# Graph attention over gathered rows: whole-array columns and value transposes, and another order of the first layer's step

## The chip, the cores and the metric

The kernel runs on one NeuronCore of a Trainium2 chip. The metric is the device time of one execution in microseconds, as the median of several runs. The engines are TensorE (PE, with its weight loads PEld), VectorE (DVE), ScalarE (ACT), GpSimd (POOL) and SyncE (SP), and 16 DMA engines that move data. [...]

## The reference

Eight graphs share one adjacency matrix of 2048 nodes; each node has 64 features. A graph attention layer with four heads is followed by a second one with one head, a layer norm, the residual and another layer norm. Scores are the inner products of a layer's features, masked by the adjacency matrix with the diagonal added:

```python
mask = graph + jnp.eye(N, dtype=graph.dtype) > 0
h = jnp.einsum('bnc,hdc->bhnd', x, Wh)
out_h = _gat_layer(h, mask[None, None], bh[None, :, None, :])      # softmax over masked h.h, times h, plus b
cat = jnp.transpose(out_h, (0, 2, 1, 3)).reshape(B, N, H * D)
z = jax.nn.leaky_relu(cat, negative_slope=0.2)
h2 = jnp.einsum('bnk,dk->bnd', z, Wo)
out2 = _gat_layer(h2, mask[None], bo)
z2 = jax.nn.leaky_relu(out2, negative_slope=0.2)
out = layernorm(z2) * gamma + beta                                 # then layernorm(x + out)
```

Here B is 8, N 2048, H 4, D and C 64, and all is float32.

## The kernel before

The adjacency matrix is sparse but for its first rows. The kernel (`fast_kernel`; a general one stands behind it for inputs that do not fit) treats the first 56 nodes, the hubs, densely, and puts the other 1992 into 166 sets of 12 nodes. For every set VectorE picks, from keys that hold a bit mask of the set's members and a node number, the up to 128 neighbours that the set has in all. These neighbours' rows are gathered from a table in device memory by an indirect DMA that GpSimd issues, and attention is done on the 128 rows alone.

There are three stages. The hub stage (to about 140 us) loads x, writes the first table, transposes x into `xT` (`turn_x`) and computes the hubs' attention, while GpSimd and VectorE turn the adjacency matrix into keys and pick neighbours. The second stage is the loop that the change is about: the first layer, 83 groups of two sets (about 145 to 625 us). The third is the second layer, from a second table that the loop writes.

One group of the first layer passes through these functions, each in another step of the software pipeline, so that a step works on some eight groups at once:

- `gather` (L797): two indirect DMAs bring 128 rows of 4 x 130 numbers each; a row holds, for each of four pairs of graphs, a one, 128 features and a one. `own_rows` (L808, L811) copies the members' own columns out of `xT` for two groups at a time, on GpSimd.
- `columns` (L819) multiplies the own columns with `gram` (Wh transposed times Wh, per head, 64x64 for each of two graphs, block diagonal in 128x128), and `keep_columns` (L826) copies the result to `y` on ScalarE. So a score is a gathered row times y.
- `turn` (L514) transposes the gathered rows, and ScalarE copies them to `xTg` (L1045).
- `scores` (L836): 16 matmuls, weights 64x128 from `xTg`, 48 columns each (12 members by 4 heads); `weigh` (L842) subtracts the mask on VectorE, `lift` (L849) takes the exponential on ScalarE.
- `values` (L861): 16 matmuls, exponentials as weights, rows of 65 numbers (features and a one, which gives the softmax's sum); `invert` (L871, L872) divides on VectorE.
- `turn_values` (L880) transposes the result, `keep_values` (L886) copies it, `project` (L538) applies the heads' Wh, `leaky` (L525) and `leak` (L530) are the leaky ReLU, `second_maps` (L895) applies Wo, `keep_own` (L900) and `store_own` (L905) keep the result, `second_rows` (L911) transposes it, and `keep_rows` (L915, L918) adds the bias and writes the second table.

The order on each engine is the order of the calls: nothing rearranges it. Semaphore waits are added where a tile is written or read by another engine. PSUM is used as four tiles of two banks each, with the tags S, C, T and O, each with one buffer. Before the change each has one reader: S is read by VectorE (scores), T by ScalarE (columns, transposed rows), C by ScalarE (project, transposed values) and O by VectorE (second_maps, values, second_rows). Most matmuls of a step use a part of the array: "64*64" in a profile's row is a tile of 64 rows and 64 columns, four of which are in the array at once. A float32 matmul stands in the profile as two records, a transpose as one.

`some` pops jobs of neighbour picking for later sets from a list and issues them on VectorE; `more` loads and converts a piece of the adjacency matrix; `make_keys` makes keys; `hub_later` finishes the hubs in three jobs for each half; `load_own` and `add_beta` prepare a third table (x + beta) for the end of layer two, by SP's DMAs and GpSimd.

Of the kernel before, what the change touches and what calls it, by code (L numbers as in the profile page):

```python
# [44 lines left out]
HUB = 56  # L45
# [314 lines left out]
def fast_kernel(ctx: ExitStack, tc: tile.TileContext, x, adj, Wh, bh, Wo, bo, gamma, beta, out, flag):  # L360
# [29 lines left out]
    rowp = stage.enter_context(tc.tile_pool(name="rowp", bufs=12))  # L390
# [118 lines left out]
    def turn(tp, rows, j=0):  # L509

        for q in range(Q):
            c0 = (j * Q + q) * 64
            for r in range(2):
                nc.tensor.transpose(tp[:, r, c0:c0 + 64], rows[half(r), q, 1:1 + P], ident[half(r), half(r)])  # L514

    def turn_whole(tp, rows):

        for q in range(Q):
            nc.tensor.transpose(tp[:, q * P:(q + 1) * P], rows[:, q, 1:1 + P], ident)  # L519
# [12 lines left out]
    def project(ot, cat, n):  # L532

        for hp in range(HP):
            for s in range(2):
                for j in range(2):
                    h = 2 * hp + j
                    at = nc.tensor.matmul(cat[half(j), s, hp * n:(hp + 1) * n], whT[half(s), h * D:(h + 1) * D],  # L538
                                          ot[half(s), h, :], start=True, stop=True)
        return at  # L540
# [47 lines left out]
    def turn_x(i):  # L588
        tp = two(f"px{i}")
        turn(tp, xrow[i])  # L590
        nc.scalar.copy(xT[:, :, i * P:(i + 1) * P].rearrange("c q (r n) -> c r q n", r=2),
                       tp[:, :, :Q * 64].rearrange("c r (q n) -> c r q n", q=Q))
# [141 lines left out]
    def pick(r):  # L734
# [7 lines left out]
        def top(src, dst, last):  # L742
            todo.append(lambda: nc.vector.max(out=dst, in_=src))
            if not last:
                todo.append(lambda: nc.vector.match_replace(out=src, in_to_replace=dst, in_values=src, imm_value=-1.0))

        for j in range(ns):
            for i in range(KEEP // 8):
                k = j * KEEP + i * 8
                top(kv[:, j, :], cand[:, k:k + 8], i == KEEP // 8 - 1)  # L750
# [7 lines left out]
        for i in range(P // 8):  # L758
            top(cand, best[:, i * 8:(i + 1) * 8], i == P // 8 - 1)
# [35 lines left out]
    def gather(table, s, layer, new, behind=None):  # L795
        t = rows[layer, s] = new(f"g{layer}_{s}")
        g = nc.gpsimd.indirect_dma_start(out=t.rearrange("n q c -> n (q c)"), out_offset=None, in_=table,  # L797
                                         in_offset=bass.IndirectOffsetOnAxis(ap=index[:, s:s + 1], axis=0))
        if behind is not None:
            tc.add_manual_dep(g.ins, behind.ins.name, mybir.DependencyInfo(mybir.DependencyClass.Sync, mybir.DependencyReason.DATA),  # L800
                              reason="the gather's turn")

    def own_rows(m):

        t = held["x", m] = work.tile([P, 2 * GM], F32, tag="xo", name=f"xo{m}", bufs=2)
        v = t.rearrange("c (b s q k) -> c b s q k", b=2, s=2, q=Q)
        src = xT[:, :, HUB:].rearrange("c q (k s) -> c s q k", s=NS)
        nc.gpsimd.tensor_copy(v[:, 0], src[:, 4 * m:4 * m + 2])  # L808
        b0 = min(4 * m + 2, NS - 2)
        for r in range(2):  # L810
            nc.gpsimd.tensor_copy(v[half(r), 1], src[half(1 - r), b0:b0 + 2])  # L811

    def columns(g, tp):

        t = held["x", g // 2]
        for k in range(2):
            for r in range(2):
                for p in range(2):
                    nc.tensor.matmul(tp[half(p), r, k * GM:(k + 1) * GM], gram[half(r), g % 2 * 2 + k, half(r)],  # L819
                                     t[half(r), (p ^ r) * GM:((p ^ r) + 1) * GM], start=True, stop=True)  # L820

    def keep_columns(g, tp):
        if g % 2 == 0:
            held["y", g // 2] = work.tile([P, 2 * GM, H], F32, tag="yg", name=f"y{g // 2}", bufs=2)
        h0 = g % 2 * 2
        nc.scalar.copy(held["y", g // 2].rearrange("p (b n) h -> p b n h", b=2)[:, :, :, h0:h0 + 2],  # L826
                       tp[:, :, :2 * GM].rearrange("p b (k n) -> p b n k", k=2))

    def scores(g, sp):
        xt = held.pop(("T", 1, g))  # L830
        y = held["y", g // 2].rearrange("p n h -> p (n h)")
        for j in range(2):
            for q in range(Q):
                for p in range(2):
                    c0 = ((g % 2) ^ p) * GM * H + (j * Q + q) * M
                    at = nc.tensor.matmul(sp[:, p, (q * 2 + j) * M:(q * 2 + j + 1) * M], xt[half(p), j, q, :],  # L836
                                          y[half(p), c0:c0 + M], start=True, stop=True)
        return at
# [12 lines left out]
    OW = D + 2  # L851

    def values(g, op):
        e = es[g % 2]
        rw = [rows.pop((1, 2 * g + j)) for j in range(2)]
        for q in range(Q):
            for j in range(2):
                for p in range(2):
                    c0 = (p * 8 + q * 2 + j) * M
                    o0 = q * OW + p  # L860
                    at = nc.tensor.matmul(op[half(p), j, o0:o0 + K1], e[:, c0:c0 + 64], rw[j][:, q, sums(p)], start=True, stop=True)  # L861
                    if (q, j, p) == (1, 1, 1):
                        midway = at
        return midway

    def invert(g, op):
        v = op[:, :, :Q * OW].rearrange("a j (q c) -> a j q c", q=Q)
        osb = held["o", g] = work.tile([P, 2, Q, D], F32, tag="osb", name=f"osb{g}")
        r = rall[:, g, :].rearrange("a (j q) -> a j q", j=2)
        for p in range(2):  # L870
            nc.vector.reciprocal(r[half(p)], v[half(p), :, :, p * K1])  # L871
        nc.vector.tensor_tensor(osb, v[:, :, :, 1:K1], r.unsqueeze(3).to_broadcast([P, 2, Q, D]), OP.mult)  # L872

    def turn_values(g, pt):

        osb = held.pop(("o", g)).rearrange("a j q c -> a (j q c)")
        for w in range(4):
            for p in range(2):
                mine = slice(p * 64, p * 64 + M)
                at = nc.tensor.transpose(pt[:, p, w * M:(w + 1) * M], osb[mine, w * P:(w + 1) * P], ident[mine, mine])  # L880
        return at

    def keep_values(g, pt):

        ot = held["ot", g] = work.tile([P, H, GM], F32, tag="ot", name=f"otb{g}")
        nc.scalar.copy(ot.rearrange("c h (p m) -> c p h m", p=2), pt.rearrange("c p (m h) -> c p h m", h=H))  # L886
# [14 lines left out]

    def store_own(g):

        t = held["own", g]
# [3 lines left out]
    def second_rows(g, pr):  # L908
        t = held.pop(("own", g))
        for r in range(2):  # L910
            nc.tensor.transpose(pr[:, r, :], t[half(r)], ident[half(r), half(r)])  # L911

    def keep_rows(g, pr):
        r = rowts[g % 4]
        nc.vector.tensor_tensor(r[:GM, 1:1 + P].rearrange("n (p d) -> n p d", p=2), pr, bob[:GM], OP.add)  # L915
# [63 lines left out]
    for i in range(NB):  # L979
# [16 lines left out]
        for t in range(2):  # L996
# [12 lines left out]
            some(6)  # L1009
# [4 lines left out]
    for g in range(3):  # L1014
# [23 lines left out]
    for i in range(-4, NG + 4):  # L1038
        if i >= 1 and slow and len(slow) % 3:
            slow.pop(0)()  # L1040
        sp = one(f"s{i + 1}", "S")
        scored = scores(i + 1, sp) if 0 <= i + 1 < NG else None
        if 0 <= i + 2 < NG:
            t = held["T", 1, i + 2] = work.tile([P, 2, Q, P], F32, tag="xTg", name=f"xTg{i + 2}", bufs=2)
            nc.scalar.copy(t.rearrange("c j q (r n) -> c r (j q) n", r=2),  # L1045
                           held.pop(("tp", i + 2)).rearrange("c r (m n) -> c r m n", n=64))
        cat = one(f"cat{i}", "C")
        if 0 <= i - 2 < NG:
            project(held.pop(("ot", i - 2)), cat, GM)
            held["z", i - 2] = leaky(cat, GM, f"z{i - 2}")  # L1050
        if 0 <= i + 1 < NG:
            weigh(i + 1, sp)
        coming = i + LOOK if i > -3 else NG
        if coming < NG:
            gather(table1, 2 * coming, 1, rows_tile, scored)
        if turns():
            some(1)
        if i >= 0:
            if slow and len(slow) % 3 == 0:
# [4 lines left out]
        tp = one(f"t{i + 3}", "T")  # L1064
        if 0 <= i + 4 < NG + NG % 2:
            columns(i + 4, tp)
            keep_columns(i + 4, tp)
        if 0 <= i + 1 < NG:
            lift(i + 1)
        op = one(f"o{i}", "O")  # L1070
        if 0 <= i - 3 < NG:
            second_maps(i - 3, op[:, 0, 264:264 + GM])
        midway = values(i, op) if 0 <= i < NG else None
        if coming < NG:
            gather(table1, 2 * coming + 1, 1, rows_tile, midway)
        if 0 <= i - 4 < NG:
            second_rows(i - 4, op[:GM, :, 360:424])
        if 0 <= i - 2 < NG:
            leak(held["z", i - 2])
        if 0 <= i - 3 < NG:  # L1080
            keep_own(i - 3, op[:, 0, 264:264 + GM])
            store_own(i - 3)
        if i + 6 < NG and i % 2 == 0 and i >= -2:
            own_rows((i + 6) // 2)
        if i >= 10 and (i - 10) // 6 * 2 + (i - 10) % 6 // 2 <= NV and (i - 10) % 6 < 4:
            (add_beta if i % 2 else load_own)((i - 10) // 6 * 2 + (i - 10) % 6 // 2)
        if 0 <= i < NG:
            invert(i, op)
        if 0 <= i - 4 < NG:
            keep_rows(i - 4, op[:GM, :, 360:424])  # L1090
        for _ in range(6 if i < 0 else 3 if i < 16 else 2):
            if not turns():
                some(1)
        if not picks:
            ready = done
        if not picks and not todo3 and done < NS:
            picks = pick(2)
            done = NS
        assert i + 1 + LOOK >= NG or 2 * (i + 1 + LOOK) + 1 < ready
# [357 lines left out]
```

## Time and profile before

| | |
|---|---|
| runs | 906.34, 915.76, 911.70 us; median 911.7 |
| profiled execution | 906.34 us; its span 904.5 us |
| TensorE clock granted, mean | 0.924 |
| first layer's loop, first to last subtraction L842 | 156.1 to 611.7 us |
| gathers (L797) | 332 of 994 ns each on GpSimd |
| DMA | 145 MB, mean 160 GB/s |

In the profile a row such as "L836 PE MATMUL s<-y,xTg 64*128 64x48 f32 x2656" names the line, the engine, the operation, the tile written and those read, the tile of the array (weights' rows by columns), the moving operand's size, and how many such records there are. A share of busy time is an average over stages; what bounds a stage is read from that stage's windows and from the chain of waits in it.

### The profile page before, as it was taken

What the parts mean: (1) busy time and instruction counts of PE and PEld (TensorE: products, weight loads), DVE (VectorE), ACT (ScalarE), POOL (GpSimd) and SP (SyncE); (2) the same over time, 40 slices, a digit from 0 to 9 for tenths busy, and PEclk for the clock granted to TensorE, in tenths of its full rate; (3) what the DMA queues carried; (4) which work ended last, traced back from release to release, by engine and by line L of the source; (5) the groups of instructions that cost most, each with busy time, mean ns of one, the idle gap of its engine ahead of it and who ended that gap; (6) DMA issues with size and microseconds to landing.
All of it is one profiled execution on the core that took longest, in us unless ns stands there. A gap on an engine that the chain in (4) does not pass through costs nothing.

```text
span 904.5 us, 40409 instructions
## 1 busy us (share of the span) xinstructions
PE 769.5 (85%) x17676; PEld 698.0 (77%) x17676; DVE 615.1 (68%) x1369; ACT 513.4 (57%) x878; POOL 487.5 (54%) x696
## 2 busy tenths in 40 slices
PE   2896776889889999999999999994799999998720
PEld 2675565778779999999999999993699989997720
DVE  3347867447677787767655556655338899999993
ACT  2332243345446666666666666662477887887721
POOL 5643140436555566655556665631777777777300
PEclk9998797669999999999999999997799999999965
DMA  8786350335444555555445455431888888888521
GB/s 176 227 239 201 107 149 4 98 101 146 112 129 130 143 142 148 149 156 143 136 127 153 140 152 153 138 83 43 255 273 248 268 263 270 270 252 249 170 49 30
DMA packets 81787, 145.11 MB, mean 160 GB/s; under 512 B 30146, under 2 KB 46466, under 8 KB 81602
## 3 DMA queue, kind: packets, MB, share of 16 engines
q0 software_dynamic: 26720, 88.55, 34.3%
q1 hardware_dynamic: 37842, 49.65, 18.0%
q10 hardware_dynamic: 17040, 4.25, 2.5%
q8 instruction: 140, 2.29, 1.0%
q14 instruction: 45, 0.37, 0.1%
HBM read 123.91 MB, written 18.48 MB: 157 GB/s over the span
## 4 chain that ended last, share of the span: by engine, by line
PE 61%; DVE 14%; DMA 11%; issue 4%; ACT 4%; POOL 2%; SPq 2%; DVEq 0%; POOLq 0%; ACTq 0%
PE s L836 15%; PE o L861 8%; DMA g<-table,index 5%; PE t L514 4%; PE t L819 4%; PE o L895 4%; PE cat L538 4%; DMA raw<-in_adj_dram 4%; PE t L519 4%; PE s L1156 3%; PE o L1188 3%; PE sh L1300 2%; PE cat L880 2%; PE e L1167 2%; PE o L911 2%
## 5 line engine op out<-in xcount | busy, mean ns | idle before, releaser
L797 POOL DMA_INDIRECT g<-table,index x332 | 330.1, 994 | 136.6 <-issue 54.3
L836 PE MATMUL s<-y,xTg 64*128 64x48 f32 x2656 | 169.6, 280 | 0.8 <-DVE rowt L660 0.8
L836 PEld LDWEIGHTS s<-y,xTg 64*128 64x128 f32 x2656 | 164.0, 197 | 1.7 <-DVE rowt L660 1.2
L842 DVE TENSOR_TENSOR e<-s,mask 128x768 f32<-128x768 f32 x83 | 79.3, 956 | 50.7 <-PE s L836 47.5
L525 ACT ACTIVATE z<-cat,bhp 128x192 f32<-128x192 f32 x166 | 60.9, 418 | 84.6 <-PE cat L538 79.3
L861 PE MATMUL o<-g,e 128*64 128x65 f32 x2656 | 96.5, 228 | 0.0
L519 PE MATMUL t<-ident,g 128*128 128x128 f32 x664 | 82.0, 277 | 12.8 <-DMA g<-table,index 12.8
L861 PEld LDWEIGHTS o<-g,e 128*64 128x64 f32 x2656 | 91.3, 144 | 0.6 <-issue 0.4
L811 POOL COPY xo<-xT 64x96 f32<-64x96 f32 x84 | 30.1, 359 | 113.5 <-DMA g<-table,index 101.5
L1343 ACT COPY xTg<-t 128x1024 f32<-128x1024 f32 x83 | 80.1, 1016 | 17.1 <-PE t L519 16.5
L1045 ACT COPY xTg<-t 128x1024 f32<-128x1024 f32 x83 | 84.4, 1017 | 2.9 <-PE t L514 2.9
L519 PEld LDWEIGHTS t<-ident,g 128*128 128x128 f32 x664 | 75.0, 143 | 14.2 <-issue 9.1
L849 ACT ACTIVATE e<-e,shifts 128x768 f32<-128x768 f32 x83 | 78.1, 941 | 0.7 <-DVE e L842 0.7
L886 ACT COPY otb<-cat 128x384 f32<-128x384 f32 x83 | 39.8, 479 | 66.5 <-PE cat L880 66.5
L604 ACT ACTIVATE e<-e,shifts 128x896 f32<-128x896 f32 x32 | 33.3, 1042 | 74.6 <-DVE e L601 65.2
L687 POOL TENSOR_SCALAR a<-raw 120x1024 bf16<-120x1024 int32 (+1 forms) x34 | 38.4, 1133 | 65.2 <-DMA raw<-in_adj_dram 36.4
L900 DVE COPY own<-o 128x96 f32<-128x96 f32 x83 | 21.3, 257 | 69.6 <-PE o L911 64.2
L530 DVE SCALAR_TENSOR_TENSOR z<-z 128x384 f32<-128x384 f32 x83 | 49.7, 599 | 27.3 <-ACT z L525 23.9
L819 PE MATMUL t<-xo,gram 64*64 64x96 f32 x1328 | 54.8, 260 | 14.2 <-DVE keys L715 5.3
L826 ACT COPY y<-t 128x384 f32<-128x384 f32 x83 | 43.5, 524 | 28.6 <-PE t L819 28.4
L514 PE MATMUL t<-ident,g 64*128 64x64 f32 x1328 | 57.9, 230 | 1.9 <-ACT y L826 1.9
L872 DVE TENSOR_TENSOR osb<-o,rall 128x512 f32<-128x512 f32 x83 | 57.4, 692 | 2.9
(171 smaller groups left out, 1488.3 us busy)
## 6 DMA issues: line engine op xcount, KB each, us to landing
raw<-in_adj_dram SPq DMA_DIRECT2D x32, 480.0 KB
table<-xb SPq DMA_DIRECT2D x22, 256.0 KB
xr_s<-table SPq DMA_DIRECT2D x21, 256.0 KB
g<-table,index POOLq DMA_INDIRECT x332
table<-x SPq DMA_DIRECT2D x16, 260.0 KB
x<-in_x_dram ACTq DMA_DIRECT2D x32, 128.0 KB
table<-rowt SPq DMA_DIRECT2D x166, 24.4 KB
xb<-in_x_dram SPq DMA_DIRECT2D x164, 24.0 KB
```

The lines of the kernel that those rows point to most:

```text
L514: nc.tensor.transpose(tp[:, r, c0:c0 + 64], rows[half(r), q, 1:1 + P], ident[half(r), half(r)])
L519: nc.tensor.transpose(tp[:, q * P:(q + 1) * P], rows[:, q, 1:1 + P], ident)
L525: nc.scalar.activation(z[:, hp], cat[:, :, hp * n:(hp + 1) * n], AF.Identity, bias=bhp[:, hp:hp + 1], scale=1.0)
L797: g = nc.gpsimd.indirect_dma_start(out=t.rearrange("n q c -> n (q c)"), out_offset=None, in_=table, in_offset=bass.IndirectOffsetOnAxis(ap ...
L819: nc.tensor.matmul(tp[half(p), r, k * GM:(k + 1) * GM], gram[half(r), g % 2 * 2 + k, half(r)], t[half(r), (p ^ r) * GM:((p ^ r) + 1) * GM] ...
L836: at = nc.tensor.matmul(sp[:, p, (q * 2 + j) * M:(q * 2 + j + 1) * M], xt[half(p), j, q, :], y[half(p), c0:c0 + M], start=True, stop=True)
L842: nc.vector.tensor_tensor(e[:, :16 * M].rearrange("p (a q n) -> p a q n", a=2, q=Q), sp[:, :, :8 * M].rearrange("p a (q n) -> p a q n", q= ...
L849: nc.scalar.activation(e[:, :16 * M], e[:, :16 * M], AF.Exp, bias=shifts[:, 0:1], scale=1.0)
L861: at = nc.tensor.matmul(op[half(p), j, o0:o0 + K1], e[:, c0:c0 + 64], rw[j][:, q, sums(p)], start=True, stop=True)
L872: nc.vector.tensor_tensor(osb, v[:, :, :, 1:K1], r.unsqueeze(3).to_broadcast([P, 2, Q, D]), OP.mult)
L1045: nc.scalar.copy(t.rearrange("c j q (r n) -> c r (j q) n", r=2), held.pop(("tp", i + 2)).rearrange("c r (m n) -> c r m n", n=64))
L1343: nc.scalar.copy(t, tp)
```

## The change

In `turn_x` the transposes use the whole array. `own_rows` copies the own columns of a pair of groups in one copy, without the second, swapped half. `columns` becomes two matmuls over 128 rows with the block-diagonal gram and 192 columns, which go into tile C. `turn_values` becomes four transposes of 112 rows into free columns of tile O, where `values` also writes, and `keep_values` two copies. `second_maps` and `second_rows` write into C, and `second_rows` is one whole transpose. So C is read by ScalarE (project, columns) and VectorE (second_maps, second_rows), O by VectorE (values) and ScalarE (transposed values). The scores and the transposes of gathered rows stay as they were in size, but the latter are split in two parts with `turn_values` between them. The gathers lose their explicit waits for `scores` and for the middle of `values`; the pool of gathered rows has 10 buffers for 12. The pipeline is shorter: project runs one step after values, second_maps two, second_rows three (two, three and four before). A picking job is now a maximum together with its replacement, two jobs a step from step 0 on (later three in two steps), where single operations stood, six a step before step 0 and then three or two. `load_own` and `add_beta` begin at step 30, not 10.

```diff
-    rowp = stage.enter_context(tc.tile_pool(name="rowp", bufs=12))
+    rowp = stage.enter_context(tc.tile_pool(name="rowp", bufs=10))
...
     def turn_x(i):
         tp = two(f"px{i}")
-        turn(tp, xrow[i])
+        turn(tp[:, 0, :], xrow[i])
...
     def own_rows(m):
-        v = t.rearrange("c (b s q k) -> c b s q k", b=2, s=2, q=Q)
-        nc.gpsimd.tensor_copy(v[:, 0], src[:, 4 * m:4 * m + 2])
-        for r in range(2):
-            nc.gpsimd.tensor_copy(v[half(r), 1], src[half(1 - r), b0:b0 + 2])
+        nc.gpsimd.tensor_copy(t[:, :w * 48].rearrange("c (s q k) -> c s q k", s=w, q=Q), src)
...
         for k in range(2):
-            for r in range(2):
-                for p in range(2):
-                    nc.tensor.matmul(tp[half(p), r, k * GM:(k + 1) * GM], gram[half(r), g % 2 * 2 + k, half(r)],
-                                     t[half(r), (p ^ r) * GM:((p ^ r) + 1) * GM], start=True, stop=True)
+            nc.tensor.matmul(cat[:, k, 2 * GM:2 * GM + n], gram[:, g % 2 * 2 + k, :], held["x", g // 2][:, :n], start=True, stop=True)
...
         for w in range(4):
-            for p in range(2):
-                mine = slice(p * 64, p * 64 + M)
-                at = nc.tensor.transpose(pt[:, p, w * M:(w + 1) * M], osb[mine, w * P:(w + 1) * P], ident[mine, mine])
+            nc.tensor.transpose(turned(op)[:, w, :], osb[:112, w].rearrange("a s c -> a (s c)"), ident[:112, :112])
...
-        for r in range(2):
-            nc.tensor.transpose(pr[:, r, :], t[half(r)], ident[half(r), half(r)])
+        nc.tensor.transpose(pr, held.pop(("own", g)), ident)
```

The loop's body after the change, cut to its order:

```python
for i in range(-4, NG + 3):
    scores(i + 1, sp); weigh(i + 1, sp)
    hub_later's jobs, all but the first of three
    project(i - 1) into cat; leaky(i - 1)
    xTg(i + 2) <- tp; lift(i + 1)
    values(i, op); invert(i, op)
    gather(2 * (i + 5)); gather(2 * (i + 5) + 1)
    own_rows for i + 6, i + 7 (even i); load_own or add_beta (from i = 30)
    leak(i - 1)
    slots of some, hub_later's first job, more(1), make_keys
    second_maps(i - 2, cat); second_rows(i - 3, cat); columns(i + 4, cat)
    keep_own(i - 2); keep_rows(i - 3)
    some(2)
    keep_columns(i + 4, cat)
    turn_halves(tp, first set of i + 3)
    turn_values(i, op); keep_values(i, op)
    turn_halves(tp, second set of i + 3)
```

## The prediction

> **What bounds the kernel now.** I read the page's busy shares first, then windows of the first layer's loop, then the chain of waits inside one of its steps, then who waits for whom.
>
> ```profile
> PE 769.5 (85%) x17676; PEld 698.0 (77%) x17676; DVE 615.1 (68%) x1369; ACT 513.4 (57%) x878; POOL 487.5 (54%) x696
> ```
>
> TensorE has the largest share, but the average mixes stages. The change touches the first layer's loop (83 groups; the scores' subtraction L842 runs 83 times, from 156.1 to 611.7 us) and, with one line, the hub stage before it. So I asked for the loop's windows (columns: busy time and instructions of PE, PEld, DVE, ACT, POOL; then granted clock, DMA share, GB/s):
>
> ```profile
> 156.00:205.00 49.00, 42.55 (x670) 37.77 (x670) 22.64 (x58) 18.84 (x32) 21.07 (x29) 0.66 0.33 94
> 205.00:275.00 70.00, 61.84 (x1421) 56.23 (x1419) 50.25 (x129) 36.67 (x66) 39.43 (x61) 0.93 0.45 126
> 275.00:430.00 155.00, 153.83 (x3969) 145.12 (x3965) 117.96 (x310) 103.54 (x183) 93.16 (x143) 1.00 0.52 146
> 430.00:600.00 170.00, 168.31 (x4250) 157.73 (x4250) 100.20 (x234) 111.06 (x197) 103.21 (x159) 0.99 0.50 141
> ```
>
> From 275 us on PE is 99% busy at full clock and no other engine is above 77%: PE is the bound. Before 205 us the clock is 0.66, so the same work takes longer there. The chain of waits of one undisturbed step says what PE's time consists of:
>
> ```profile
> 461.74 1.79 PE s L836 x32
> 463.53 0.49 PE cat L538 x16
> 464.02 0.33 PE t L819 x16
> 464.35 0.48 PE o L895 x8
> 464.83 0.93 PE o L861 x32
> 465.76 0.19 PE o L911 x2
> 465.95 0.54 PE t L514 x16
> 466.49 0.24 PE cat L880 x8
> 466.73 1.79 PE s L836 x32
> ```
>
> The chain never leaves PE, and the step lasts 466.73 - 461.74 = 4.99 us; most steps in the trace are 4.94 apart. L538 and L819 are the same 16 instructions of 64x64 by 96 columns, but the first costs 0.49 and the second 0.33: L538 is first after the scores, which run as 64x128 tiles. So a switch between tile shapes costs 0.16. L895 repeats it: its 8 records cost 0.48, as 4 pairs at the pace of L819's quartets (0.33 / 4) cost 0.33, and they follow a switch to 128x64. The third switch, back to 64x128, is in L911. Three switches a step now.
>
> Steps 273.3 to 602.6 us are 64; at 4.94 they would take 316, so 13 us are lost, mostly in every second step. Steps 156.1 to 273.3 are 16, 117 us in place of 79: 38 lost. Who waits:
>
> ```profile
> POOL xo L811 <- DMA g<-table,index: 99.2, 34, 3.8
> ...
> PEld t L819 <- POOL xo L811: 7.6, 18, 2.2
> ```
>
> The second copy of own_rows waits on POOL until the gathers in flight have landed, and L819 then waits for it.
>
> **The change, part by part.** In the new step PE issues: scores (64x128), project (64x64), values and second_maps (128x64), second_rows and columns (128x128), turn_halves of the first set (64x128), turn_values (128x128), turn_halves of the second set (64x128). That is six switches, not three.
> - Scores, project: as now, 1.79 + 0.49.
> - Values take over the switch into 128x64 from second_maps: 0.93 + 0.16 = 1.09; second_maps 0.33.
> - Full-array transposes. The second layer has them: its chain shows
>
> ```profile
> 748.89 0.59 PE e L1167 x4
> 749.47 1.75 PE t L519 x16
> ```
>
>  1.75 / 16 = 0.11 each, and four of them after a switch 0.59 (4 x 0.11 + 0.15, the switch again). turn_values becomes four such: 0.59 for 0.24. second_rows becomes one after a switch: 0.26 for 0.19.
> - Columns: 2 matmuls with 192 columns over 128 rows, four records for sixteen. No 192-column pass is in the trace. The nearest is the hub scores' L598 (224 columns), whose pairs of passes start 0.19 apart in the trace (the chain gives x8 0.96 with the switch: (0.96 - 0.16) / 4 = 0.20). By columns, 0.163 a pass, 0.65 in all, for 0.33 now. Lower bound 4 x 0.11 (the 128-column transposes), upper 4 x 0.20; I take 0.65, as 192 is nearest to 224.
> - turn_halves: the 16 records of L514 take 0.49 in the steps beside this one; split in two by turn_values, each half pays a switch: 2 x (0.245 + 0.16) = 0.81.
>
> [...]
>
> Sum of the new step: 1.79 + 0.49 + 1.09 + 0.33 + 0.26 + 0.65 + 0.59 + 0.81 = 6.01, against 4.94 now: +1.07, over 82 steps **+88 us**.
>
> What covers the other engines, in time from the step's start. invert waits for values (done near 3.5), takes 0.41 + 0.69 (L871, L872) and ends near 4.75; turn_values is reached at 5.0: cover 0.25. second_maps writes the bank pair that leaky reads, so it waits for ScalarE: project ends near 2.4, leaky takes 0.73, so 3.25; PE arrives at 3.4: cover 0.15. turn_halves needs the xTg copy (1.02) behind leaky: 4.3, PE arrives at 4.75. keep_columns now waits for VectorE too, because keep_own and keep_rows read the same pair of banks: leak, own, rows end near 5.85, keep_columns (0.52) and keep_values, now two copies (2 x 0.37, as L525's 0.73 for two of that size), end at 7.2; the next project comes at 6.01 + 1.95 = 7.96. Behind the waiting keep_columns only keep_values is queued. All hidden, so nothing is charged; if cover fails by 0.2 a step it costs 16 us.
>
> [...]
>
> VectorE: 0.96 + 0.41 + 0.69 + 0.56 + 0.26 + 0.28 = 3.16 a step, and now two picks of a maximum and a replacement each (0.43 + 0.09 + 0.41, some 0.98 with gaps) for the first 22 steps, where single operations stood: 5.1, under 6.01. POOL: two gathers at 1.28 with their issue, own_rows one copy, add_beta 1.26 every other step: under 4. The gathers now wait for values, at 3.5, are issued by 6.1 and, by the 3.8 us that the copy L811 waits behind them at most, land by 10; turn_halves wants them two steps on, at 16.8. Ten row buffers instead of twelve are covered by that. load_own and add_beta start 20 steps later; SP issues load_own's eight DMAs in 3.35 us (at 463.9), every second step, so the two DMAs of keep_rows behind them still fit a step and have four row buffers; table3 is read only in layer two. The jobs of hub_later move behind the scores and their subtraction: to_table then waits for the subtraction, about 1.1 us, where now the scores wait for its row (L660, 0.4 us); it runs twice, 1 to 2 us, within the rounding of what follows.
>
> What is removed: L811's wait. The 13 us of 64 steps hold 2 for a step with a table of indices (6.8 us, stays); the other 11 are its, and so are 5 of the step at 222 us (10.1 us long: PE idle 1.98 behind L811, then half clock): **-16**. The first steps' other 33 us (hub_later, make_keys, half clock) stay; some ten steps at clock 0.66 make the added 1.07 half as dear again: +5. turn_x: four full transposes for eight halves, 0.44 for 0.24, and a switch more, 16 times 0.36 = 6; the hub stage waits for ScalarE and VectorE too, so half: +3. The drain is a step shorter: -2.
>
> Total: 88 - 16 + 5 + 3 - 2 = **+78**. The profiled execution took 906.3 (span 904.5 and 1.8 around it): 984. It was the fastest of three; their median is 911.7, and from that it would be 990. I say **985**, nearer the execution that the sum is made from.
>
> **Rivals.**
> 1. PE is bound as above, with small terms off: 962 to 1000. 66%.
> 2. The thin covers fail: second_maps, turn_halves or turn_values wait 0.2 to 0.4 each step, and idle brings half clock as it did at 222 us. For it: covers of 0.15 to 0.25, and 0.56 us of leak that once took 1.4 at 299 us. Against: the PE queue has slack after a wait. 985 + 16 to 33 = 1001 to 1018. 14%.
> 3. The new switches are cheaper (full-height tiles load their weights early): three at 0 in place of 0.16 is -39: 946; half of that 966. Against: L1167 pays 0.15 right there. 14%.
> 4. Not slower: a switch's cost is no drain but the order of banks, and vanishes wherever the next operation has another pair of banks. Then all six are free, also the three paid now: 6.01 - 0.96 = 5.05, +0.11 x 82 = 9, with -16 and +6: 905, or 911 from the median. It decides if a switch costs under 0.03 (six of them are then 0.2 a step). Against: L538 and L819 write different banks and only the first pays. 4%. That the change does otherwise than it says (2%) I exclude by the built order, which has these instructions.
>
> **The numbers.** The range 950 to 1010 holds rival 1, half of 2 and most of 3. Faster by over 1% (about what a measurement of this kernel tells from no change): 0.03, the better half of 4 and the unknown; within 1%: 0.03; slower: 0.94.
>
> **What would show it.** Right: steps 5.9 to 6.1 us apart between 300 and 600 us, PE still 98% busy at clock 1.00, columns near 0.65, turn_values near 0.59, two pieces of turn_halves near 0.4 each, no wait of POOL's xo copy for gathers. Wrong: columns at 0.33; switch steps without the extra 0.15; PE idle before second_maps, turn_halves or turn_values; VectorE over 95% in the first 45 steps; or a clock under 0.9 after 275 us.

## The result, and the profile after

The changed kernel takes 956.09 us (median of 4 runs, 952.12 to 959.59) where the kernel before takes 913.73 in the same measurement (4 runs, 906.34 to 920.58): ratio 1.049, 95% interval 1.040 to 1.058. Its profiled execution took 958.55 us, with a span of 956.7 beside 904.5 before: +52.2 where the forecast had +78. The profiled execution of before was its fastest run, so the medians lie only 42 us apart. On another chip the sign was the other one; that is in the experiments (f1 and f2).

The page of the kernel after, busy time by engine:

```profile
PE 832.6 (87%) x16189; PEld 721.6 (75%) x16189; DVE 611.8 (64%) x1369; ACT 514.8 (54%) x961; POOL 464.1 (49%) x612
```

TensorE has 1,487 matmul records fewer (a float32 matmul makes two) and is busy 63 us longer. The windows of the first layer's loop, columns as before:

```profile
156.00:205.00 49.00, 44.28 (x684) 37.98 (x680) 24.19 (x62) 20.69 (x44) 20.09 (x27) 0.80 0.34 93
205.00:275.00 70.00, 66.22 (x1215) 56.51 (x1210) 55.15 (x142) 36.90 (x75) 33.22 (x47) 1.00 0.41 111
275.00:430.00 155.00, 154.33 (x2959) 135.16 (x2961) 106.10 (x288) 88.78 (x182) 73.17 (x97) 1.00 0.43 118
430.00:600.00 170.00, 169.33 (x3248) 148.09 (x3244) 88.86 (x215) 98.41 (x201) 89.63 (x114) 1.00 0.50 139
```

PE is 99.6% busy at full clock from 275 us on, and gets through 2959 records in 155 us where before got through 3969. Ahead of 275 us its clock is higher than before's (0.80 for 0.66, 1.00 for 0.93). The chain of waits through one step:

```profile
464.63 1.77 PE s L825 x32
466.40 0.49 PE cat L538 x16
466.89 1.08 PE o L850 x32
467.98 0.33 PE cat L884 x8
468.31 0.24 PE cat L894
468.55 0.65 PE cat L811 x4
469.20 0.40 PE t L514 x8
469.60 0.53 PE o L867 x4
470.13 0.39 PE t L514 x8
470.52 1.77 PE s L825 x32
```

It never leaves PE. Read down the column beside the forecast's terms: scores 1.77 (1.79), project 0.49, values 1.08 (1.09), second_maps 0.33, second_rows 0.24 (0.26), columns 0.65, halves 0.40 and 0.39 (0.405 each), turn_values 0.53 (0.59). The step is 5.89 us (6.01), and 57 of the 60 steps from 18 to 77 lie within 0.12 of it. Last, who waits for whom between 200 and 640 us (total, times, longest):

```profile
POOL g L797 <- PE o L850: 194.5, 74, 5.8
...
ACT y L817 <- DVE rowt L898: 56.4, 72, 4.3
```

The gathers wait for values (`L850` here), and keep_columns (`L817`) waits for VectorE, as the forecast had it; nothing on PE waits behind either. No wait of the copy of own_rows for gathers is left.

So the span's +52.2 comes from these stretches (us; a step is the distance between two of the scores' subtractions):

| stretch | before | after | difference | the forecast implied |
|---|---|---|---|---|
| to the first subtraction | 156.1 | 154.1 | -2.0 | +3 |
| steps -1 to 14 | 117.2 | 115.7 | -1.5 | 16 x 1.07 + 5 - 5 = +17 |
| steps 15 to 80 | 338.4 | 390.1 | +51.7 | 66 x 1.07 - 11 = +60 |
| behind the last subtraction | 292.8 | 296.8 | +4.0 | -2 |

### The profile page after: what moved, and what is told of

Read it like the earlier page. It is cut to its first block, busy times and chain, and to the rows that moved or that the text cites. A ratio compares the mean times of both kernels' runs of the same rounds, so it can differ in the third digit from the quotient of the medians.

```text
span 956.7 us, 37570 instructions
## 1 busy us (share of the span) xinstructions
PE 832.6 (87%) x16189; PEld 721.6 (75%) x16189; DVE 611.8 (64%) x1369; ACT 514.8 (54%) x961; POOL 464.1 (49%) x612
## 4 chain that ended last, share of the span: by engine, by line
PE 70%; DVE 12%; DMA 4%; ACT 4%; issue 4%; POOL 2%; SPq 2%; ACTq 1%; DVEq 0%; POOLq 0%
PE s L825 16%; PE o L850 9%; PE t L514 7%; PE cat L811 6%; PE o L867 5%; PE cat L538 4%; PE t L519 4%; PE s L1137 3%; PE cat L884 3%; PE o L1169 3%; PE cat L894 2%; PE e L1148 2%; PE sh L1281 2%; ACT xTg L1324 1%; SPq L1252 1%
## 5 line engine op out<-in xcount | busy, mean ns | idle before, releaser
L825 PE MATMUL s<-y,xTg 64*128 64x48 f32 x2656 | 164.1, 274 | 0.0
L825 PEld LDWEIGHTS s<-y,xTg 64*128 64x128 f32 x2656 | 158.6, 192 | 0.1
L525 ACT ACTIVATE z<-cat,bhp 128x192 f32<-128x192 f32 x166 | 60.8, 418 | 154.1 <-PE cat L538 154.1
L850 PE MATMUL o<-g,e 128*64 128x65 f32 x2656 | 99.1, 229 | 0.0
L850 PEld LDWEIGHTS o<-g,e 128*64 128x64 f32 x2656 | 87.3, 142 | 10.0 <-issue 0.4
L514 PEld LDWEIGHTS t<-ident,g 64*128 64x128 f32 x1328 | 54.8, 140 | 33.1 <-issue 20.9
L514 PE MATMUL t<-ident,g 64*128 64x64 f32 x1328 | 77.2, 238 | 2.4 <-issue 2.4
L817 ACT COPY y<-cat 128x384 f32<-128x384 f32 (+1 forms) x80 | 40.9, 511 | 61.9 <-DVE rowt L898 59.0
L857 DVE RECIPROCAL rall<-o 64x8 f32<-64x8 f32 x166 | 34.0, 205 | 58.3 <-PE o L850 57.1
L811 PE MATMUL cat<-xo,gram 128*128 128x192 f32 (+1 forms) x320 | 65.7, 328 | 0.0
L811 PEld LDWEIGHTS cat<-xo,gram 128*128 128x128 f32 x320 | 53.7, 202 | 0.2 <-issue 0.2
L1169 PE MATMUL o<-g,es 128*32 128x65 f32 x2656 | 48.2, 224 | 5.0 <-DVE y_s L1192 4.5
```

The lines of the kernel that those rows point to most:

```text
L525: nc.scalar.activation(z[:, hp], cat[:, :, hp * n:(hp + 1) * n], AF.Identity, bias=bhp[:, hp:hp + 1], scale=1.0)
L811: nc.tensor.matmul(cat[:, k, 2 * GM:2 * GM + n], gram[:, g % 2 * 2 + k, :], held["x", g // 2][:, :n], start=True, stop=True)
L1169: nc.tensor.matmul(op[t * 32:(t + 1) * 32, f, k * W2 + p:k * W2 + p + K1], e[:, 2 * q + p, k, :], rw[:, q, sums(p)], start=(a == 0 and k = ...
```

## The experiments

The theory (A in what follows): PE's own time sets the step, and the added time is in the switches between tile shapes and in the columns. The rivals go by run. Runs e1 to e4 shared a chip (before: 920.73 us median, 13 runs, 911.29 to 929.98). The record doesn't say whether the first measurement fell on it too; "the first chip" below stands for both.

**e1, columns alone.** Before, with whole-array columns and one copy in own_rows (still into tile T):

```diff
-                    nc.tensor.matmul(tp[half(p), r, k * GM:(k + 1) * GM], gram[half(r), g % 2 * 2 + k, half(r)],
-                                     t[half(r), (p ^ r) * GM:((p ^ r) + 1) * GM], start=True, stop=True)
+            nc.tensor.matmul(cat[:, k, 0:n], gram[:, g % 2 * 2 + k, :], held["x", g // 2][:, :n], start=True, stop=True)
```

> The kernel before with one part of the change: columns as two whole-array matmuls of 192 columns (into tile T, as before), and own_rows as one copy; nothing else. Theory A (PE is the bound, a switch of tile shape costs 0.15, a pass of 192 float32 columns 0.163): columns cost 0.65 in place of 0.33 and there is one switch more (64x64 to 128x128 to 128x64), so steps lie 5.4 apart in place of 4.94, +39 us over 82 steps; the copy no longer waits for gathers, -16; so 23 us slower than before, ratio 1.02 to 1.03. Rival B (a switch costs nothing in itself, the added time comes from the waits between engines): step 5.26, +26 - 16 = +10. Rival C (the lost waits weigh more than the array work): faster than before, ratio under 1.00, with the half-clock stretches before 275 us shorter.

Measured: 932.44 us (931.16 to 933.58), ratio 1.012 (1.004 to 1.019). That is 11.7 us between the medians, which by itself would be rival B's +10; the span, 931.3, is 26.8 above before's profile. The steps decide: 5.46 us, flat (A: 5.4, B: 5.26), and the copy of own_rows waits for no gather. From its chain of waits:

```profile
459.21 0.49 PE cat L538 x16
459.70 0.85 PE t L814 x4
460.55 0.48 PE o L887 x8
```

Four records take 0.85 where sixteen took 0.33: 0.65 of work, as in the kernel after, and 0.20 for the switch. That is +0.52 a step, and the wait it takes away gives part of it back. Against e4 below, which lacks that wait too, e1 is 33.8 us slower (medians), and its steps 15 to 80 take 359.5 us for 326.7: 0.50 a step.

**e2, turn_values ahead of both halves.** After, with the first `turn_halves` moved behind `turn_values`: two switches less, as turn_values follows columns in the same shape and the second half follows the first; and less time for VectorE's invert.

```diff
-            turn_halves(tp, rows[1, 2 * (i + 3)], 0)
         if 0 <= i < NG:
             turn_values(i, op)
             keep_values(i, op)
         if 0 <= i + 3 < NG:
+            turn_halves(tp, rows[1, 2 * (i + 3)], 0)
             turn_halves(tp, rows[1, 2 * (i + 3) + 1], 1)
```

> The changed kernel with one thing moved: turn_values stands right after columns, and both parts of turn_halves follow it. Theory A: two of six switches go (turn_values stays in the 128x128 shape, the second half follows the first), 0.27 a step, but PE then reaches turn_values at 4.67 after the scores' start, when VectorE's division is just ending (4.70 in the trace), so 0.1 to 0.2 of it becomes a wait: steps 5.72 to 5.80 in place of 5.89, 8 to 14 us faster than the changed kernel; without any wait 22. Rival B (switches are free): the wait alone remains, steps 6.0 to 6.1, 8 to 16 us slower than the changed kernel.

Measured: 952.32 us (944.75 to 960.38), ratio to before 1.036 (1.027 to 1.046); steps 5.84.

```profile
465.09 0.65 PE cat L811 x4
465.74 0.03 issue
465.77 0.60 PE o L867 x4
466.37 0.64 PE t L514 x16
```

The two halves together take 0.64 where they took 0.40 + 0.39: a switch is worth 0.15. But turn_values now takes 0.60, for the wait for invert that the first half had covered: between 200 and 640 us its weight loads wait 69 times for VectorE's division, 22.0 us in all, where the kernel after has no such wait. So the step gains 0.05 only, outside of what either theory gave, nearer to A. The first half did cover invert there, as the forecast had it.

**e3, values turned in row tiles.** After, with `turn_values` as eight transposes in row tiles and one `keep_values` copy, as before the change (values and invert then lay out tile O as before, too):

```diff
-            nc.tensor.transpose(turned(op)[:, w, :], osb[:112, w].rearrange("a s c -> a (s c)"), ident[:112, :112])
+            for p in range(2):
+                mine = slice(p * 64, p * 64 + M)
+                nc.tensor.transpose(turned(op)[:, p, w * M:(w + 1) * M], osb[mine, w * P:(w + 1) * P], ident[mine, mine])
```

> The changed kernel with turn_values again as eight transposes of 48 rows in 64x128 tiles, into tile O (one bank for each row half), and keep_values as one copy; the order is unchanged. Theory A: turn_values costs 0.24 in place of 0.53 and the two switches around it go, so turn_halves, turn_values, turn_halves cost 0.39 + 0.24 + 0.25 = 0.88 in place of 1.32: steps 5.45 in place of 5.89, 36 us faster than the changed kernel, about 920. Rival B (only the transposes' width counts): 0.44 becomes 0.24, steps 5.69, 16 us faster.

Measured: 920.70 us (10 runs, 912.91 to 925.94), ratio to before 1.001 (0.996 to 1.005), some 35 us below the 956.09 of the kernel after, which was measured apart. Steps 5.46. From its chain:

```profile
469.25 0.65 PE cat L811 x4
469.91 0.39 PE t L514 x5
470.30 0.24 PE o L868 x5
470.53 0.26 PE t L514 x7
```

turn_values takes 0.24 for 0.53, and the second half 0.26 for 0.39: a switch less at each of the two places, and less work in the first. The step is 0.43 shorter, so rival B (5.69) falls; with e1's 0.52 that is 0.95, all of 5.89 - 4.94. (Some records are missing in this view; the times are those of whole groups.)

**e4, the swapped copy on VectorE.** Before, with only the engine of the copy L811 changed:

```diff
-            nc.gpsimd.tensor_copy(v[half(r), 1], src[half(1 - r), b0:b0 + 2])
+            nc.vector.tensor_copy(v[half(r), 1], src[half(1 - r), b0:b0 + 2])
```

> The kernel before with one thing moved: the two swapped copies of own_rows run on VectorE, where they wait for no gather; GpSimd keeps the first copy. Theory A (the copy's wait behind the gathers made columns late, and the pause left PE at half clock for some us): 11 us of the 64 steps after 273 us and 5 us of the step at 222 us go, so 12 to 18 us faster than before, ratio 0.98 to 0.985, and no step after 300 us over 5.3 but the one with a table of indices. Rival B (the lost time of the early steps also hangs on that wait): 25 to 35 us faster, with the half-clock stretches between 145 and 205 us shorter as well. Rival C (VectorE's queue makes the copies late in its place): no gain.

Measured: 898.66 us (890.97 to 906.16), ratio 0.970 (0.960 to 0.979); steps are 4.94 flat from step 48 on. The 22 us between the medians lie between A's 12 to 18 and B's 25 to 35. In the profiles steps 15 to 80 are 11.7 us shorter than before's and steps -1 to 14 4.2 us, 16 in all, as A counted; where the other 6 come from isn't shown. So the wait that the change removed was to be had without the change, at 371 ns on VectorE each (mean from 300 to 600 us), and this kernel is faster than both.

The next eight runs fell on two other chips, on which all is slower: e5 to e8 on one (before: 1098.56 median, 23 runs, 1084.6 to 1113.15), f1 to f4 on another (before: 1110.27, 7 runs, 1104.11 to 1117.32). They are compared only there.

**e5, gathers without their explicit waits**, as the change has them:

```diff
-            gather(table1, 2 * coming, 1, rows_tile, scored)
+            gather(table1, 2 * coming, 1, rows_tile)
```

(and `midway` likewise).

> The kernel before with one part of the change: the gathers without their explicit waits for scores and for the middle of values (12 row buffers, order of calls and all else as before). Theory A (the copy L811 waits until the gathers issued in the same step have landed, 3.8 us behind them): issued at the step's start, they land before store_own has let the copy come up, the copy's wait falls under 2 us and columns are no longer late: steps of 4.94 after 300 us throughout, 10 to 20 us faster than before. Rival B (GpSimd's order, not the waits, sets the copies' time): L811's wait stays near 3 us a pair and the time does not move.

Measured: 1127.40 us (1124.25 to 1139.87), ratio 1.028 (1.021 to 1.036): both theories missed the time. The copy's wait did fall as A had it, to 15 waits of 2.2 us at most (300 to 650 us). But PE pauses in values, about once a step, with no wait in the trace (waits from 300 to 600 us):

```profile
PEld o L861 <- issue: 32.4, 65, 1.2
...
PE o L861 <- issue: 23.4, 62, 1.1
```

**e6, the hub row behind the scores** (`to_table` moved past scores and weigh, as in the change), and **e7, picks in pairs** as in the change.

```diff
-        if i >= 1 and slow and len(slow) % 3:
+        if i >= 1 and slow and len(slow) % 3 == 2:
             slow.pop(0)()
...
+        if i in (2, 4):
+            slow.pop(0)()
```

> The kernel before with one part of the change: hub_later's third job (to_table, twice) stands behind the scores and their subtraction, not ahead of the scores. Theory A (the early steps of the changed kernel lose some 7 us less than those of before, because the scores wait less for to_table and the clock comes back sooner): steps 2 and 4 shorter by 1 to 3 us each, half clock after 170 us 3 to 7 us less, in all 3 to 7 us faster. Rival B (where the half clock lasts is a matter of the clock's own windows, and the order of this job does not matter): within 3 us of before.

```diff
-        for _ in range(6 if i < 0 else 3 if i < 16 else 2):
+        for _ in range((2 if i < 22 or i % 2 else 1) if i >= 0 else 0):
```

> The kernel before with one part of the change: picking jobs as pairs of a maximum and a replacement, two a step from step 0 (later three in two steps), none before step 0. Theory A (PE is the bound; VectorE has room): VectorE then has 5.1 us of work in a step of 4.94, so for the first 22 steps with picks the subtraction comes late and steps lie near 5.2 to 5.4 apart, 5 to 10 us slower; later none. Rival B (the picks before step 0 keep the first scores waiting): the first steps are shorter, 3 to 8 us faster in all.

Measured: e6 1100.99, ratio 1.003 (0.999 to 1.007); e7 1101.16, ratio 1.003 (0.999 to 1.006). On this chip neither part of the change moves the time by more than 0.7%: as rival B had it for e6, and as neither theory had it for e7. That agrees with the forecast, which charged nothing for them; on the first chip they weren't run alone.

**e8, a better kernel**: e4's copy, make_keys and the hubs' jobs in tile S, `to_table` split so that the scores needn't wait for its row.

```diff
-        return one(name, "T")
+        return one(name, "S")
...
-        return [turn_back, through_heads, to_table]
+        return [turn_back, through_heads, to_table, hub_row]
```

> The kernel before with the swapped copies of own_rows on VectorE (as e4), and with make_keys and the picked indices' transpose in tile S, which is free once the subtraction is done, in place of T, for which columns waits; to_table split so that its transpose stands behind values. Theory A: e4's gain of 16 to 30 us, and in steps 10, 12 and 14 the wait of columns for VectorE's keys (2.6 us each in steps 10 and 14) goes, 4 to 8 us more, with 2 to 3 us at to_table: 885 to 895. Rival B (what is taken from these waits comes back as the next subtraction waiting behind the keys on VectorE): as e4 alone, near 898.

Measured: 1061.53 us (6 runs, 1051.23 to 1064.59), ratio 0.964 (0.959 to 0.969). Beside e4's 0.970 on the first chip the rest of it isn't shown to add anything.

**f1 and f2, before and after once more**, for a second profile of each.

> The kernel before, a second profile of it. Question: the forecast of the early steps (steps -1 to 14) was 18.5 us too high, and the profiled execution of before had 54.5 us at clock 0.50 between 111 and 275 us against 30.7 in after. Theory A: the half clock stretches belong to the kernel (its early waits), so a second profile of before shows 45 to 65 us of them again and steps -1 to 14 within 4 us of 117. Rival B: they fall by chance, so this profile shows under 40 or over 70 us of them and steps -1 to 14 off by over 5 us.

> The changed kernel, a second profile of it and a ratio on another chip. The spacing of steady steps is 5.89 us in any case if it is TensorE's own work. Theory A (half clock belongs to the kernel): 25 to 36 us at half clock between 111 and 275 us and steps -1 to 14 within 4 us of 116, ratio to before 1.04 to 1.06. Rival B (chance): half clock outside 20 to 42 us, steps -1 to 14 off by over 5 us; the ratio then moves with it, anywhere from 1.03 to 1.08.

Of the question, half clock between 111 and 275 us: 54.8 and 63.8 us in the two profiles of before, 34.1 and 30.9 in those of after, as A had it. Steps -1 to 14 of before are 123.3 (6 off, as B had it), of after 112.2 (within A's 4). The other runs say the same of whole executions. An estimate from each run's span and mean clock (time at half clock is twice the missing share of the span, as the clock in the traces of before and after is 1.00 or 0.50 and nothing between) gives 89 to 113 us in after and 131 to 180 in before on the first chip, 141 to 161 and 221 to 289 on this one. So the difference belongs to the kernel, and its size varies from run to run. The ratio was expected by neither: after 1087.78 us (1085.60 to 1091.45), before 1110.27 (and 1113.11 in f1's four runs, 1093.52 to 1122.94), ratio 0.981 (0.975 to 0.987). On this chip the change is some 2% **faster**. The windows from 275 to 430 us, first f1, then f2:

```profile
275.00:430.00 155.00, 145.15 (x3228) 132.67 (x3230) 97.26 (x248) 85.20 (x150) 79.78 (x120) 0.90 0.45 123
```

```profile
275.00:430.00 155.00, 154.33 (x2917) 135.18 (x2915) 106.62 (x290) 91.19 (x182) 72.02 (x96) 0.99 0.43 115
```

The kernel after does here what it did on the first chip (2917 records for 2959, steps of 5.89). The kernel before falls from 3969 records to 3228, and its steps 15 to 80 from 338.4 us to 392.2; after's take 392.6. So the loop's loss is gone, since before lost the same by other means. The rest of f2's gain (steps -1 to 14: -11.1; behind the last subtraction: -15.8 of 433.1) is from one profile each, and f1's is of one of its slower executions (1114.35 us). The 15.8 lie in the second layer, whose code the change doesn't touch, and are not explained.

**f3 and f4, e5 and e8 once more.**

> The kernel before without the two explicit waits of the gathers, as in e5, which was 2.8% slower, with TensorE pausing in the middle of values. Theory A: the explicit waits keep the gathers off the second copy of own_rows and off VectorE's work; without them it is slower on any chip: ratio 1.02 to 1.04 again, and steps between 300 and 600 us over 5.1 us on average. Rival B: the loss was that chip's, whose TensorE queue was often empty: here the ratio is within 0.99 to 1.01 and steady steps are 4.94 us.

> The kernel before with the swapped copy of own_rows on VectorE, make_keys and the slots in tile S, and to_table split (as e8). Theory A: as e8's 0.964, and e4's 0.970 for the copy alone: 0.96 to 0.975 here, steady steps 4.94 us with none above 5.2 after the picks have ended. Rival B: it depended on the chip: 0.98 or more.

Measured: f3 1137.90 us, ratio 1.020 (1.011 to 1.030), as e5; but this chip stalls as that one did, so what the explicit waits are worth on the first chip stays open. f4 1063.60 us (1057.73 to 1065.21), ratio 0.957 (0.950 to 0.964), its steps from 18 to 77 5.44 on average, not A's 4.94. f4 has before's matmuls without the wait of L811 and at clock 1.00, so it shows most simply what is lost on this chip. Its chain of waits:

```profile
507.50 0.48 PE o L899 x8
507.98 0.22 PE o L865 x7
508.20 0.18 issue
508.38 0.97 PE o L865 x25
...
513.02 0.48 PE o L899 x8
513.50 0.23 PE o L865 x7
513.72 0.08 issue
```

PE stops once a step inside values, with nothing to wait for ("issue": 14.9 us in 48 waits of its weight loads from 275 to 600 us). The stops (PE's starts over 0.25 us apart) are mostly 127 to 131 matmul records from one another, or parts that add up to that. The queue that carries instructions (packets, MB, share of 16 engines' time, from 275 to 600 us) says what else has this period; first f4, then e4, then the kernel after:

```profile
q8 instruction: 61, 1.00, 1.3%
```

```profile
q8 instruction: 67, 1.10, 1.4%
```

```profile
q8 instruction: 49, 0.80, 1.0%
```

In f4 61 packets of 16 KB come for 7752 matmul records: one for 127, and one every 5.35 us on average. On the first chip e4 takes one every 4.86 us, and has no such stops. The kernel after needs one every 6.66 us there and 6.70 on f2's chip, and has no stops with this period on either. So it may be that on these chips PE's instructions came at one packet in some 5.3 us, and that a loop which issues fewer of them isn't held up. This is argued, not shown: no run changed the supply of instructions alone, and the rate isn't a fixed bound (from 602 us on, at the end of f4's loop, five packets come 4.87 us apart on average). It suits f4 and e8, but not every run. In e5 a packet is needed only every 6.3 us, an estimate at those 127 records to one (7046 records from 250 to 600 us), and PE stops in values all the same, as in f3 (32.4 and 32.0 us in 65 and 66 waits of the weight loads). In f1 before's stops lie mostly in the scores and the columns, and ScalarE waits for a release that the trace can't name (f1, waits from 300 to 650 us):

```profile
ACT otb L886 <- remote: 40.2, 15, 3.0
```

f2, f4 and the profiles on the first chip show no such wait from 275 to 600 us. Before also spends 51.2 us at half clock in this stretch in f1 (3.4 on the first chip, 0.0 in f4), worth half of that by an estimate, about 0.39 a step (the 32 records of the scores at 197.2 us in before, at 0.50, take 3.65 us, those at 466.6, at 1.00, 1.95). With 0.45 for the stops (f4's 5.40 against e4's 4.95 over steps 15 to 80) this adds up to its step's rise from 5.13 to 5.94; but f1's own stops aren't f4's, so the sum fits without showing the split. What slows before on this chip stays open.

## Why the prediction was right, and where it was off

- **PE as the bound, and the sum of its step**: right. +0.95 a step, shown in two parts by e1 (0.52) and e3 (0.43). The term of 1.07 was 0.12 too large, half of it in turn_values (0.59 forecast from the second layer's L1167, 0.53 measured): 8 us over steps 15 to 80.
- **A switch costs 0.16**: right (0.15 in e2, 0.13 in e3's second half, 0.15 ahead of values, 0.20 ahead of e1's columns). Rivals 3 and 4, cheaper or free switches, fall by this.
- **Columns by the row of 224 columns**: right, 0.65 for the four passes in the chain of the kernel after, as in those of e2 and e3.
- **Covers of 0.15 to 0.25 us**: they held (windows 99.6% busy). Rival 2 falls; e2 shows that the one ahead of turn_values was needed.
- **L811's wait, -16**: right. It is gone as said, and e4, which takes away that wait alone, has steps that are 16 us shorter in its profile (11.7 and 4.2); between the medians it gains 22 us (920.73 to 898.66).
- **"The first steps' other 33 us stay"**: this step failed. Steps -1 to 14 cost 1.5 us less than before, where +17 was implied. The forecast left half clock as it was and added 5 us for dearer work under it; instead half clock inside these steps fell from 43.8 to 21.3 us (54.8 to 34.1 between 111 and 275 us), worth 11 us. These 16 and some 2 for the smaller step make up the miss. f1 and f2 show that the fall belongs to the kernel. Which part of the change does so isn't told apart. Between 111 and 275 us there are 47.9 us with the columns alone (e1), 57.2 without the copy's wait (e4), 61.1 with free gathers (e5), 63.8 with the hub row later (e6) and 60.0 with paired picks (e7), so none of these alone does it. The kernel after without the values' part keeps it low (37.5, e3), and with turn_values moved by one place it is lower still (17.1, e2). What is left is the rest of the change: the order of the step, its tiles and the shorter pipeline; no run takes these apart.
- **Hub stage +3**: it was -2; the dearer transposes forecast for turn_x aren't seen in the time (the last ends at 130.0 us, before at 131.0). **Drain -2**: it was +4 with what follows. From the last subtraction to the second layer's first gather it is 20.0 us, before 17.8: the last steps wait for VectorE (osb, 0.70) and ScalarE (otb, 0.55) with no other group beside them. The other 1.8 lie in the second layer.

These misses (-8, -18.5, -5, +6) make 78 into 52. All but the last lie on the same side, so the central value was 29 us above the median, still inside the range. The median, 956.09, lies 6 us above the range's lower end and below rival 1's own band (962 to 1000), where half of rival 3's cheaper switches would have put it, though the switches were not cheaper. That the range held is in part luck: its low end was there for a reason that didn't come true.

- **What the forecast didn't ask**: whether before's time holds on another chip. Its 130 matmul records a step, 26 a us, are what the two other chips didn't keep up, whatever the reason; the change's 113 in 5.89 us ran on f2's chip as on the first. "Slower" is shown for the first chip alone.

## What to carry to other kernels

Price a step by its runs of equal tile shape: each border cost 0.13 to 0.20 us here, so a rewrite that makes fewer and larger matmuls can lose if it puts different shapes beside one another; and ask whether the wait that it removes can be had alone, as one copy on another engine did here (-3%). Where PE is the bound, count its instructions too, and measure on more than one chip: a loop at 26 matmul records a us ran at full speed on one chip and took 16% longer on another, and the kernel with fewer instructions, slower on the first, was the faster there. That the count is the reason is argued only.

## What was unexpected of the hardware

- The copy L811 on GpSimd, with a shift between partitions, waits until the gathers in flight have landed (3.8 us at most); on VectorE (e4) it doesn't. The trace of before has this wait as instructions of GpSimd's queue, so it stands in the program as built:

```profile
L811 POOLq EVENT_SEMAPHORE  x83: 17/43/3873, 129.1 to 594.6; - x83
```

  The copy L808 beside it, without a shift, has one such record. Whether the hardware needs the wait no run shows.
- Half clock came in whole pieces: in before's profile, between 111 and 275 us, 3.4, 6.8, 10.2 and 23.9 us (one, two, three and seven times 3.41), each after pauses of PE. The piece at 223.8 us sets in during a pause of 1.98 us, and one of 3.4 us at 452.5 us follows a pause of 0.47 us, the only one over 0.2 us in the 10 us ahead of it. Both pauses are shorter than one such piece. Which pauses bring one no run shows.
- The same program takes 906 to 930 us on the first chip and 1085 to 1123 on two others. The part behind the loop is 433.1 us in f1 and 292.8 in the first profile; in windows of it DMA moves 131 to 160 GB/s in f1 and 235 to 269 in the first. Why these chips are slower isn't shown by any run.
